# Loading six fields of one tile in parts of 39, 40 and 49 rows in a DMA-bound pairwise-product kernel

## The chip, the cores and the metric

The kernel runs on one core of a Trainium2 chip. Times are device microseconds (us) of that core, as medians of several executions; every execution that is compared here was in the fast state, with a granted TensorE clock of 0.535 to 0.548 in the profiled ones. A profile is one further execution.

## The reference

```python
# r_x: (4096, 32, 64) float32;  W: (64, 64) float32
vid = x @ W                                   # per field
out[:, pair(i, j), :] = x[:, i, :] * vid[:, j, :]   # all i < j: 496 pairs
# out: (4096, 496, 64) float32, 520 MB
```

(The two lines are the reference's content in short form.) The output is fifteen times the input: this is a problem of writing.

## The kernel before

The batch is cut into 16 tiles of 256 rows. A tile of x lies in SBUF as 128 partitions (two halves of the batch by 64 embedding positions) by 32 fields by 128 rows. (SBUF is the on-chip memory that DMA transfers fill and empty, PSUM the memory that TensorE writes.) TensorE makes `vid` for a tile in PSUM, VectorE multiplies, and SyncE issues the store of each finished piece. There are two x buffers and three output buffers.

```python
xpool = ctx.enter_context(tc.tile_pool(name="x", bufs=2))
opool = ctx.enter_context(tc.tile_pool(name="out", bufs=3))
...
def load(t, pieces, queue):
    xt = xpool.tile([P, F, C], F32, tag="x", name=f"x_{t}")
    n = F // pieces
    for lo in range(0, F, n):
        queue.dma_start(out=xt[:, lo : lo + n, :], in_=x[t][:, lo : lo + n, :])
    return xt

loaded = [load(0, 4, nc.sync), load(1, 2, nc.sync)]
...
for t in range(NT):
    if 0 < t < NT - 1:
        loaded.append(load(t + 1, 4, nc.scalar))
    xt = loaded[t]
    ...                                       # matmuls: vid
    for at, m, w, i, di, j, dj in products(by_field() if t < 2 else by_block()):
        ...
        nc.vector.tensor_tensor(o, left, right, ALU.mult)
        ...
        nc.sync.dma_start(out=out[t][:, sent:at, :], in_=ot[:, sent - base : at - base, :])
```

From tile 2 on a store moves 128 rows of 63,488 bytes. Each of the sixteen DMA engines takes eight of these rows, and each adds one step to the store's completion semaphore, the counter by which the program learns that a transfer has landed, after its eighth.

Of the kernel before, what the change touches and what calls it, by code (L numbers as in the profile page):

```python
# [1 line left out]

# [4 lines left out]

F32 = mybir.dt.float32
ALU = mybir.AluOpType

P = 128

C = 128

SLOT = 124

PAD = 8

GROWING = [
    21, 15, 19, 23, 27, 19, 29, 18, 19, 20, 38, 28, 24, 25, 47, 34, 29, 61,  # L20
    55, 69, 66, 58, 77, 47, 93, 31,
]


def by_field():

    return [("row", j, 0, 1, j) for j in range(1, 32)]


def by_block():  # L30


    def within(lo):
        yield "step", lo, 2, 1, 0
        for k in range(2):
            yield "step", lo, 4, 2, k
        for i in (lo, lo + 8):
            yield "row", i + 4, i, 4, 4
        yield "row", lo + 8, lo, 8, 8

    yield from within(0)
    yield "row", 16, 0, 16, 16
    yield from within(16)


def products(blocks):

    at = 0
    for kind, a, b, c, d in blocks:

        if kind == "row":
            rows, n, i0, di, j0, dj = c, d, b, 0, a, 1
        else:
            rows, n, i0, di, j0, dj = 16 // b, c, a, b, a + c + d, b
        r = k = 0
        while r < rows:
            room = SLOT - at % SLOT
            if k or room < n:
                m, w = 1, min(n - k, room)
            else:  # L60
                m, w = min(rows - r, room // n), n
            yield at, m, w, i0 + r * di + k, di, j0 + r * dj, dj
            at += m * w
            if w == n or k + w == n:
                r, k = r + m, 0
            else:
                k += w


def pairs(blocks):  # L70

    for at, m, w, i, di, j, dj in products(blocks):
        for r in range(m):
            for k in range(w):
                yield i + r * di + k, j + r * dj


@with_exitstack
def pairwise_bilinear_kernel(
    ctx: ExitStack,  # L80
    tc: tile.TileContext,
    x: bass.AP,
    w: bass.AP,
    out: bass.AP,
):




    nc = tc.nc  # L90
    NT = x.shape[0]
    F = x.shape[2] - PAD
    D = P // 2
    NP = F * (F - 1) // 2

    BANK = 512 // C


    ctx.enter_context(tc.manual_schedule(engines={mybir.EngineType.SP}))

    const = ctx.enter_context(tc.tile_pool(name="const", bufs=1))
    xpool = ctx.enter_context(tc.tile_pool(name="x", bufs=2))
    opool = ctx.enter_context(tc.tile_pool(name="out", bufs=3))
    psum = ctx.enter_context(
        tc.tile_pool(name="ps", bufs=1, space=bass.MemoryType.PSUM)
    )
    vid = psum.tile([P, F, C], F32)


    w2 = const.tile([P, D], F32)  # L110
    nc.sync.dma_start(out=w2, in_=w)  # L111
# [5 lines that stand above are left out]
            queue.dma_start(out=xt[:, lo : lo + n, :], in_=x[t][:, lo : lo + n, :])  # L117
        return xt

    loaded = [load(0, 4, nc.sync), load(1, 2, nc.sync)]  # L120

    done = 0
    growing = iter(GROWING)
    until = next(growing)
# [6 lines that stand above are left out]
        for b in range(0, F, BANK):  # L131
            for h in range(2):
                half = slice(h * D, (h + 1) * D)
                nc.tensor.matmul(  # L134
                    vid[half, b : b + BANK, :],
                    lhsT=w2[half, :],
                    rhs=xt[half, b : b + BANK, :],
                    start=True,
                    stop=True,
                )  # L140

        sent = 0
        for at, m, w, i, di, j, dj in products(by_field() if t < 2 else by_block()):
            base = at - at % SLOT
            if at == base:
                ot = opool.tile([P, SLOT, C], F32, tag="o", name=f"o_{t}_{at}")
            n = m * w
            o = ot[:, at - base : at - base + n, :]
            if m == 1:
                left = xt[:, i : i + w, :]  # L150
                right = vid[:, j : j + 1, :].to_broadcast([P, w, C])
            else:
                o = o.rearrange("p (m w) c -> p m w c", m=m)
                right = vid[:, j : j + (m - 1) * dj + 1 : dj, :].unsqueeze(2).to_broadcast([P, m, w, C])
                if di == 0:
                    left = xt[:, i : i + w, :].unsqueeze(1).to_broadcast([P, m, w, C])
                else:
                    left = xt.rearrange("p (m d) c -> p m d c", d=di)[:, i // di : i // di + m, i % di : i % di + w, :]
            nc.vector.tensor_tensor(o, left, right, ALU.mult)  # L159
            at += n  # L160
            if t * NP + at == until or at in (base + SLOT, NP):
                nc.sync.dma_start(
                    out=out[t][:, sent:at, :],
                    in_=ot[:, sent - base : at - base, :],
                )
                sent = at
                if t * NP + at == until:
                    until += next(growing, NT * NP)


_INS = ["r_x", "L0_rec_W"]
_OUTS = [((4096, 496, 64), "float32")]


# [36 lines left out]
```

## Time and profile before

| | before |
|---|---|
| median of the first 3 runs | 1293.61 us (1291.99 to 1294.53) |
| profiled run, time / span | 1295.21 us / 1293.4 us |
| DMA engines covered by packets, both data queues | 99.5% |
| VectorE busy | 1083.6 us, 84% |
| first / last of the last store's sixteen steps | 1282.40 / 1292.58 us |

The first line was all that was known of the kernel's own spread when the prediction was made. The last line is the one to remember: the sixteen engines end up to 10.2 us apart, and the kernel ends with the last of them. Below, an engine's **lag** is its step of a store behind the first engine's step of the same store. The prediction shows the lines of the profile for this.

### The profile page before, as it was taken

To read this page: it belongs to the slowest core of one execution; us is meant where nothing else is said; L and a number is where in the kernel's file an instruction comes from. 1 tells how busy PE (TensorE), PEld (TensorE's weight loads), DVE (VectorE), ACT (ScalarE), POOL (GpSimd) and SP (SyncE) were. 2 spreads that over 40 slices of the span, in tenths; PEclk is the share of its full clock that TensorE was granted. 3 is DMA by queue.
4 is the path that set the end of the run, shared out by engine and by line. 5 is a ranking of instruction groups with operands and counts; after the bars stand their busy time and mean duration, and the time that the engine had idled before them with its cause. 6 is when DMAs were issued, how large, how long until landed. Compare 5 with 4: busy or idle time off the path is not lost.

```text
span 1293.4 us, 1789 instructions
## 1 busy us (share of the span) xinstructions
PE 227.8 (18%) x512; PEld 48.5 (4%) x512; DVE 1083.6 (84%) x320; POOL 0.2 (0%) x4
## 2 busy tenths in 40 slices
PE   4112122112122121221212212122121221212000
PEld 1000000000000000000000000000000000000000
DVE  7999999888898887888879788798887988979870
POOL 0000000000000000000000000000000000000000
PEclk7555555555555565555555556555565555555555
DMA  9999999999999999999999999999999999999996
GB/s 393 429 423 438 429 432 435 430 431 434 433 434 431 432 433 435 433 435 436 433 431 436 431 433 431 435 434 431 431 431 434 431 433 427 427 431 438 438 430 302
DMA packets 20889, 553.80 MB, mean 428 GB/s; under 512 B 2448, under 2 KB 2448, under 8 KB 10256
## 3 DMA queue, kind: packets, MB, share of 16 engines
q1 hardware_dynamic: 12816, 524.33, 93.9%
q10 hardware_dynamic: 8064, 29.36, 5.6%
q8 instruction: 4, 0.07, 0.0%
q14 instruction: 5, 0.04, 0.0%
HBM read 33.59 MB, written 520.09 MB: 428 GB/s over the span
## 4 chain that ended last, share of the span: by engine, by line
DMA 55%; DVE 39%; issue 2%; PE 0%; DVEq 0%; SPq 0%
DMA out_dram<-o 55%; DVE o L159 39%; DMA x<-in_r_x_dram 0%; PE vid L134 0%; DVEq L200 0%; DVEq L159 0%; SPq L111 0%
## 5 line engine op out<-in xcount | busy, mean ns | idle before, releaser
L159 DVE TENSOR_TENSOR o<-x,vid 128x2048 f32<-128x2048 f32 (+13 forms) x320 | 1083.6, 3454 | 170.0 <-DMA out_dram<-o 124.2
L134 PE MATMUL vid<-x,w 64*64 64x512 f32 x512 | 227.8, 1025 | 958.6 <-DMA x<-in_r_x_dram 629.4
L134 PEld LDWEIGHTS vid<-x,w 64*64 64x64 f32 x512 | 48.5, 205 | 1136.2 <-DVE o L159 572.9
L182 POOL MEMSET const-bfloat16-1.0<- 128x1 bf16 x1 | 0.1, 102 | 0.0
L182 POOL MEMSET const-uint8-127<- 128x1 uint8 x1 | 0.1, 101 | 0.0
L182 POOL MEMSET const-float32-0.0<- 128x1 f32 x1 | 0.1, 99 | 0.2 <-issue 0.2
L182 POOL MEMSET const-float32-1.0<- 128x1 f32 x1 | 0.1, 98 | 0.0
## 6 DMA issues: line engine op xcount, KB each, us to landing
out_dram<-o SPq DMA_DIRECT2D x56, 7936.0 KB, 43.1
x<-in_r_x_dram ACTq DMA_DIRECT2D x56, 512.0 KB, 45.5
out_dram<-o SPq DMA_DIRECT2D x2, 3008.0 KB, 17.7
out_dram<-o SPq DMA_DIRECT2D x1, 5952.0 KB, 26.9
out_dram<-o SPq DMA_DIRECT2D x1, 4928.0 KB, 23.1
out_dram<-o SPq DMA_DIRECT2D x1, 4416.0 KB, 19.0
out_dram<-o SPq DMA_DIRECT2D x1, 4224.0 KB, 21.2
out_dram<-o SPq DMA_DIRECT2D x1, 3904.0 KB, 15.3
```

Source lines behind the costliest of these rows:

```text
L134: nc.tensor.matmul(vid[half, b : b + BANK, :], lhsT=w2[half, :], rhs=xt[half, b : b + BANK, :], start=True, stop=True,)
L159: nc.vector.tensor_tensor(o, left, right, ALU.mult)
L182: nc = _bacc.Bacc("TRN2", target_bir_lowering=False, num_devices=1, dynamic_dma_scratch_size=1024)
```

## The change

The change gives some engines more of an early load than others. Tile 1's x was two loads of 128 rows, eight rows an engine in each. Now 26 of its 32 fields are one load of 128 rows, and the other six come in parts of 39, 40 and 49 rows, which are not shared over all sixteen engines.

```diff
-    loaded = [load(0, 4, nc.sync), load(1, 2, nc.sync)]
+    loaded = [load(0, 4, nc.sync)]
+
+    x1 = xpool.tile([P, F, C], F32, tag="x", name="x_1")
+    for p, q, lo, hi in ((0, P, 6, F), (0, 39, 0, 6), (39, 79, 0, 6), (79, P, 0, 6)):
+        nc.sync.dma_start(out=x1[p:q, lo:hi, :], in_=x[1][p:q, lo:hi, :])
+    loaded.append(x1)
```

## The prediction

> **What bounds the kernel now.** I read the page first: the busy lines, the forty slices, the queue table, the grouped instructions. Busiest engine and data movement come out like this:
>
> ```profile
> PE 227.8 (18%) x512; PEld 48.5 (4%) x512; DVE 1083.6 (84%) x320; POOL 0.2 (0%) x4
> ...
> DMA  9999999999999999999999999999999999999996
> ...
> q1 hardware_dynamic: 12816, 524.33, 93.9%
> q10 hardware_dynamic: 8064, 29.36, 5.6%
> HBM read 33.59 MB, written 520.09 MB: 428 GB/s over the span
> ```
>
> VectorE has 16% to spare; the sixteen DMA engines have nothing: 93.9 + 5.6 = 99.5% of their span is covered by packets. q1 is SyncE's queue (all stores, tile 0's and tile 1's x), q10 is ScalarE's (x of tiles 2 to 15). To see where the missing share lies I cut the span into stretches. Columns: length, busy us of each engine, TensorE clock, DMA share, GB/s.
>
> ```profile
> 0.00:3.00 3.00, 0.00 (x0) 0.00 (x0) 0.00 (x0) 0.20 (x4) 1.00 0.31 60
> 3.00:12.00 9.00, 6.87 (x24) 2.35 (x26) 4.25 (x7) 0.00 (x0) 1.00 1.01 415
> 12.00:60.00 48.00, 10.65 (x34) 2.12 (x30) 48.00 (x24) 0.00 (x0) 0.57 1.01 428
> 60.00:212.00 152.00, 29.86 (x66) 5.97 (x68) 151.87 (x57) 0.00 (x0) 0.53 1.01 434
> 212.00:1280.00 1068.00, 180.48 (x392) 38.10 (x392) 879.47 (x234) 0.00 (x0) 0.54 1.00 433
> ```
>
> From 3 us on the DMA share is 1.00 or a hair over (packets overlap by some ns at hand-over). Every stretch in which something waits (VectorE for buffers, TensorE for x) is one in which the transfers run at full rate. The end is different:
>
> ```profile
> 1278.00:1280.00 2.00, 0.00 (x0) 0.00 (x0) 0.00 (x0) 0.00 (x0) 0.50 1.17 508
> 1280.00:1282.00 2.00, 0.00 (x0) 0.00 (x0) 0.00 (x0) 0.00 (x0) 0.50 0.66 286
> 1282.00:1284.00 2.00, 0.00 (x0) 0.00 (x0) 0.00 (x0) 0.00 (x0) 0.50 0.30 127
> 1284.00:1286.00 2.00, 0.00 (x0) 0.00 (x0) 0.00 (x0) 0.00 (x0) 0.50 0.29 127
> 1286.00:1288.00 2.00, 0.00 (x0) 0.00 (x0) 0.00 (x0) 0.00 (x0) 0.50 0.22 95
> 1288.00:1290.00 2.00, 0.00 (x0) 0.00 (x0) 0.00 (x0) 0.00 (x0) 0.50 0.07 32
> 1290.00:1292.00 2.00, 0.00 (x0) 0.00 (x0) 0.00 (x0) 0.00 (x0) 0.50 0.00 0
> ```
>
> (A packet counts where it begins, so the shares are coarse.) All work but the last store's data is done, and the engines finish one after another. The trace has each engine's own step of the store's completion semaphore. For the last store they fall at 1282.4 (seven engines within 0.25 us), 1284.0 to 1284.2 (four), then 1288.2, 1288.5, 1288.9, 1289.3, and the last alone at 1292.6. The first store's sixteen steps lie within 0.86 us. So one engine ends 10.2 us after the best, and the end of the kernel is that engine's end: 2.6 us of start, its packets back to back, the completion.
>
> The chain of waits says the same from the other side:
>
> ```profile
> 1197.35 39.09 DMA out_dram<-o
> 1236.49 0.04 issue
> 1236.53 0.69 DVE o L159
> 1237.22 1.13 DVEq L200
> 1238.35 15.25 DVE o L159 x5
> ```
>
> VectorE resumes at 1236.5, when the last of the sixteen steps of a store issued 39 us earlier has come (1226.3 to 1236.4).
>
> **What the Trainium skill says.** "DMA: Bandwidth & Descriptors", section "Why a DMA increments its semaphore by 16 and not by 1": the number k of engines is the largest up to 16 that divides the slowest dimension of both sides, and from the sync and scalar queues they are the lowest-numbered k. Hence 39 rows go to 13 engines (three each), 40 to 10 (four each), 49 to 7 (seven each). All transfers of the kernel before have 128 rows, so its trace can't confirm this for other counts; it agrees for 128 (sixteen steps each). Same page, "Queues, rings and completion order": an engine takes turns between queues packet by packet. The trace agrees: an x load of tile 2 or later, eight 4096-byte packets an engine, takes 45.5 us to land because each packet sits between stores of 2346 ns. Same page, "Latency and other measured facts": engines 7 and 15 are usually slower than the others; here some engines do fall behind, but the trace has no engine numbers to check which.
>
> **The change, part by part.** Bytes are equal. Removed: two loads of 128 rows by 8192 bytes. Added: one of 128 rows by 26 fields (13312 bytes) and parts of 39, 40 and 49 rows by 6 fields (3072 bytes). Packet durations in the trace: 4096 bytes 159 ns, 8192 bytes 309 ns, so 0.0366 ns a byte. Estimates from these: 13312 bytes 309 + 5120 x 0.0366 = 497 ns; 3072 bytes 159 - 1024 x 0.0366 = 122 ns.
>
> Each engine's time on this tile before: 16 x 309 = 4944 ns. After, 8 x 497 = 3976 ns plus its small rows:
> - engines 0 to 6: 3 + 4 + 7 = 14 rows, 1708 ns: 5684, that is +0.74 us
> - engines 7 to 9: 3 + 4 = 7 rows, 854 ns: 4830, -0.11 us
> - engines 10 to 12: 3 rows, 366 ns: 4342, -0.60 us
> - engines 13 to 15: none: 3976, -0.97 us
>
> The sum over sixteen is nearly 0 (5.18 - 0.33 - 1.80 - 2.91 = +0.14 us). As every engine is busy to its own end, an engine's shift at 13 us is carried to the end, and the kernel's end moves by the shift of the one engine that is last. It has 3.3 us on the next, so no other can take its place.
>
> SyncE issues two more loads at about 0.45 us each. Before, its last load was issued at 3.69 us and the first store, waiting for VectorE, at 11.14: hidden.
>
> The order of instructions shows one more effect. Eight completion semaphores are used in turn, and a DMA waits until the one eight places earlier in program order has landed. With two more DMAs the turn shifts, and the scheduler also places the loads of tile 2 slightly differently. The store issued at 84.26 us now waits for the first of those loads, which landed at 91.80; the next store waits for the second load, which was behind the first. So one store is issued about 8 us late, and its predecessor's data ends at 90.2 to 91.6. SyncE's queue would be empty for 1 to 3 us. But the other three pieces wait in ScalarE's queue: 24 packets x 159 ns = 3.8 us for each engine, which now go without stores between them. The gap is filled by work that has to be done anyway. From tile 3 on, the waits are the old ones under other names.
>
> **The rivals.**
> - The late engine is one of 13 to 15: -0.97 us, 1292.6. For: the parts give most to seven engines, and seven are the early ones at the end. Against: the trace doesn't number them.
> - It is one of 0 to 6: +0.74 us, 1294.3.
> - The engines relieved run dry in the first 30 us. For: stores there come barely in time. The fifth is issued at 22.85; from the first load's issue (1.17) to the first packets of x (about 2.3) is about 1 us, so it is ready at 23.9, and the fourth begins to land at 24.82. An engine that is 0.97 us ahead arrives at 23.85. Idle would be at most some tenths, and only an engine that is ahead has it: it reduces the -0.97, no more.
> - The late store at 84 us starves VectorE: a buffer is freed late. VectorE's later use of that buffer begins at about 128 us, and its second store landed at 112.8. With 15 us to spare I expect nothing; if the fill failed, 2 to 3 us would be lost, 1296.
> - Full balance of the lag. The mean lag of the last store's sixteen steps is (7 x 10.1 + 4 x 8.5 + 4.4 + 4.1 + 3.7 + 3.3) / 16 = 7.5 us, 0.6%. That is the most that any sharing could bring; this one moves 0.97 us.
>
> **Range and chances.** I weigh engines 13 to 15 with 0.4, 10 to 12 with 0.15, 7 to 9 with 0.2, 0 to 6 with 0.25: -0.39 - 0.09 - 0.02 + 0.19 = -0.3 us. From 1293.61: 1293.3 us. The runs of before spread from 1291.99 to 1294.53, more than the effect, so a median of a few may be 1 us off by chance; with the shift of -1.0 to +0.7 I take 1291.5 to 1295.1. Two per cent are 26 us. Nothing found comes near: full balance saves 7.5, a failed fill costs 3. Faster 0.01, within 0.98, slower 0.01.
>
> **What would show it right or wrong.** Right: in the changed kernel the three parts have 13, 10 and 7 steps that come with data and the rest at once; the steps of the first store spread over about 2 us in place of 0.86, in groups of 7, 3, 3, 3; the DMA share stays 1.00 from 3 to 1280 us, also at 84 to 95; the tile 2 loads land ten or more us earlier; the last store still has one engine some 9 to 11 us behind, within 1 us of before. Wrong: a share well under 1 anywhere between 12 and 100 us; VectorE waiting longer for buffers around 128 us; or the lag of the last engine changing by much more than 1 us, which would mean that the lag isn't carried along but depends on what the engines do together.

## The result, and the profile after

Four runs of each kernel: changed 1297.49 us median (1296.89 to 1299.03), before 1294.07 us (1291.99 to 1296.55). The ratio is 1.0027 with a 95% interval of 1.0007 to 1.0048. Ratios here are the mean time of one kernel's fast runs over that of the other's of the same rounds, so they are not quite the ratio of the medians quoted beside them. By the 2% criterion that is the same time, as predicted, but 1297.49 lies 2.4 us above the top of the predicted range.

The page of the changed kernel, its DMA slices and queues:

```profile
DMA  9999999999999999999999999999999999999995
...
q1 hardware_dynamic: 12830, 524.33, 93.7%
q10 hardware_dynamic: 8064, 29.36, 5.6%
```

The same bytes in 14 packets more; only the last slice differs. The changed kernel cut into stretches (columns as in the prediction: length, busy us of PE, PEld, DVE, POOL, TensorE clock, DMA share, GB/s):

```profile
3.00:12.00 9.00, 6.53 (x20) 2.23 (x22) 3.90 (x7) 0.00 (x0) 1.00 1.01 407
12.00:60.00 48.00, 11.89 (x38) 2.56 (x34) 48.00 (x24) 0.00 (x0) 0.59 1.01 425
60.00:120.00 60.00, 12.86 (x32) 2.68 (x32) 60.00 (x32) 0.00 (x0) 0.56 1.02 429
120.00:212.00 92.00, 15.24 (x32) 2.86 (x32) 92.00 (x26) 0.00 (x0) 0.52 1.00 432
212.00:1280.00 1068.00, 180.37 (x392) 38.16 (x392) 879.74 (x235) 0.00 (x0) 0.54 1.00 433
```

No stretch from 3 to 1280 us is idle, and VectorE is busy throughout from 12 to 212 us: it waits for no buffer there. The predicted late store is there: over 76 to 96 us SyncE's waits for a load of x, first of the kernel before, then of the changed one (in total, times, longest):

```profile
SPq L162 <- DMA x<-in_r_x_dram: 7.2, 1, 7.2
```

```profile
SPq L167 <- DMA x<-in_r_x_dram: 16.1, 2, 15.4
```

The store that was issued at 84.26 us is now issued at 92.48. In its place tile 2's loads pass, which over 70 to 130 us show as follows (last column: median us from issue to landing), before and then changed:

```profile
x<-in_r_x_dram ACTq DMA_DIRECT2D x4, 512.0 KB, 29.8
```

```profile
x<-in_r_x_dram ACTq DMA_DIRECT2D x4, 512.0 KB, 16.8
```

The pieces had landed at 91.8, 101.4, 113.0 and 124.3 us; now they land at 91.7, 93.1, 95.0 and 96.7. Chaining the packets in time (each begins within some ns of its predecessor's end on the same engine) gives whole-DMA idle time between 4 and 1270 us: 0.00 us an engine before, 0.01 after. So no engine was without a packet. But a packet can hold a wait. From 84 to 95 us the DMA share is 1.00 in both kernels while the bytes differ, before and then changed:

```profile
84.00:95.00 11.00, 3.06 (x8) 0.84 (x8) 11.00 (x8) 0.00 (x0) 0.50 1.00 426
```

```profile
84.00:95.00 11.00, 2.45 (x6) 0.84 (x8) 11.00 (x8) 0.00 (x0) 0.50 1.00 401
```

The store whose data end there has rows of 31,232 bytes. In the kernel before, fifteen of the sixteen last rows took 1156 to 1158 ns, one 1220. In the changed one, with the next store late, thirteen of them took 1352 to 2028 ns, and by and large the earlier an engine began its row, the longer the row. Over that store's 128 rows this is 0.3 us an engine more than before (0.55 against 0.24 us over 1156 ns a row). The even kernel even9, with the same late store, shows it too (0.64 us).

Otherwise the pair of profiles differs in the views at the end. The changed kernel's last 14 us:

```profile
1280.00:1282.00 2.00, 0.00 (x0) 0.00 (x0) 0.00 (x0) 0.00 (x0) 0.50 1.10 476
1282.00:1284.00 2.00, 0.00 (x0) 0.00 (x0) 0.00 (x0) 0.00 (x0) 0.50 0.44 190
1284.00:1286.00 2.00, 0.00 (x0) 0.00 (x0) 0.00 (x0) 0.00 (x0) 0.50 0.37 159
1286.00:1288.00 2.00, 0.00 (x0) 0.00 (x0) 0.00 (x0) 0.00 (x0) 0.50 0.15 63
1288.00:1290.00 2.00, 0.00 (x0) 0.00 (x0) 0.00 (x0) 0.00 (x0) 0.50 0.07 32
1290.00:1292.00 2.00, 0.00 (x0) 0.00 (x0) 0.00 (x0) 0.00 (x0) 0.50 0.07 32
1292.00:1294.00 2.00, 0.00 (x0) 0.00 (x0) 0.00 (x0) 0.00 (x0) 0.50 0.07 32
```

A share of 0.07 is the one packet of one engine of sixteen that begins in the slice. Before, it ended in the slice from 1288 us; now one engine alone starts packets for six us. The last store's steps say it exactly: first step 1283.18 (before 1282.40), last 1296.15 (before 1292.58). The first engines are 0.8 us later, and the last engine's lag is 12.97 us in place of 10.19.

**How the lag comes about.** Two things can be read from the packets, and neither was in the prediction. A store's row of 63,488 bytes takes 2342 ns. On an engine that is behind, some rows take over 2400 ns (most of these up to 2515), and mostly it is the eighth, the last row of a store: 176 of 197 such rows in the kernel before, 159 of 184 in the changed one. The share of slow last rows by the engine's lag at its step of the store before, from about 130 us on (the table needs each engine followed from packet to packet, so it is a reconstruction; the lower three rows are of kernels that are described below):

```
lag, us        0-0.3    0.3-0.8   0.8-1.5   1.5-2.3   2.3-3
before         0%       8%        64%       28%       56%
changed        0%       2%        31%       42%       67%
even9_again    1%       12%       14%       8%        10%
uneven7        2%       2%        8%        5%        17%
burden         0%       2%        16%       23%       43%
```

(In the kernel before, 1 of 453 in the first column.) The last engine of before had 52 slow rows, 42 of them eighth rows, 7.3 us in sum over 2342 ns a row; that of the changed kernel 64, 45 of them eighth rows, and 9.4 us. These sums are most of the two lags. The second thing is smaller: the page's two queues called instruction (nine packets of 8192 or 16,384 bytes in the whole run) put 0.3 or 0.9 to 1.0 us on whichever engine carries one. Slow last rows are rare at lags under 0.3 us and common in these two kernels above 0.8, but there is no fixed threshold: in burden two engines stayed at 1.0 to 1.2 us from 260 to 500 us and did not grow.

### The profile page after: what moved, and what is told of

The parts are those of the page before. It is cut to its first block, busy times and chain, and to the rows that moved or that the text cites. A ratio compares the mean times of both kernels' runs of the same rounds, so it can differ in the third digit from the quotient of the medians.

```text
span 1297.1 us, 1792 instructions
## 1 busy us (share of the span) xinstructions
PE 226.9 (17%) x512; PEld 48.5 (4%) x512; DVE 1083.6 (84%) x320; POOL 0.2 (0%) x4
## 4 chain that ended last, share of the span: by engine, by line
DMA 59%; DVE 36%; issue 2%; PE 0%; DVEq 0%; SPq 0%
DMA out_dram<-o 58%; DVE o L164 36%; DMA x<-in_r_x_dram 0%; PE vid L139 0%; DVEq L205 0%; DVEq L164 0%; SPq L111 0%
```

## The experiments

Four sets, each on one chip with eleven runs of the kernel before beside it, in alternation. The theories at the start: the imposed shares set which engine lags and how much (**sharing**, theory 1 in the recorded texts); more loads and another turn of the completion semaphores cost the time (**count**, theory 2); and, from the second set on, these kernels differ by nothing that the runs can tell (**chance**, theory 3). Theory 1' is sharing with a threshold of about 0.8 us of lag, from which an engine falls back further.

### Even parts: even9

Parts of 48, 32 and 48 rows are shared evenly by sixteen engines; everything else is as in the changed kernel, its late store included (issued at 93.03 us).

```diff
-    ... ((0, P, 6, F), (0, 39, 0, 6), (39, 79, 0, 6), (79, P, 0, 6)):
+    ... ((0, P, 6, F), (0, 48, 0, 6), (48, 80, 0, 6), (80, P, 0, 6)):
```

> The changed kernel with its three small parts cut at 48, 32 and 48 rows, so that all sixteen engines get three, two and three rows: the same bytes, sizes, number of loads and semaphore waits, shared evenly. If the uneven sharing costs the 3.4 us (theory 1: engines that start behind fall further behind), this is back at the time before, 1293 to 1295 us. If the two extra loads, the shifted semaphores and the store that is issued 8 us later cost it (theory 2), it is as slow as the changed kernel, 1296.5 to 1298.5.

1293.99 us median (1291.13 to 1297.67, 6 runs), ratio 0.9984 (0.9966 to 1.0001). The kernel before in the same rounds: 1297.21 us median, from 1290.84 to 1298.32. Two findings: more loads and the late store cost nothing that this shows, so **count** is weak; and the kernel before, whose three first runs lay within 2.5 us, spreads over 7.5.

### Fewer loads, uneven and even: uneven7, even7

Tile 0's x in two loads (8 and 24 fields) instead of four, so that the number of loads is again that of the kernel before; once with the uneven and once with the even parts.

```diff
-    loaded = [load(0, 4, nc.sync)]
+    loaded = [load_two(0)]          # fields 0-8, then 8-32
```

> The changed kernel, uneven parts included, with tile 0's x in two loads in place of four, so that seven loads come ahead of the stores as before, and no store is issued late for a load. Theory 1 (sharing): 2 to 4 us slower than before, 1296 to 1298. Theory 2 (number of loads and waits): as before, 1293 to 1295.

1297.02 us (1291.48 to 1298.76), ratio 0.9994 (0.9973 to 1.0014). The median lies where **sharing** expected it, but so does that of the kernel before in the same rounds, 1297.21.

> The control for uneven7: tile 0's x in two loads, the small parts of tile 1 shared evenly. Both theories: as before, 1293 to 1295.5; its difference to uneven7 is the sharing alone: 2 to 4 us under theory 1, under 1 under theory 2.

1295.7 us (1290.83 to 1297.72), ratio 0.9985 (0.9966 to 1.0004). The uneven kernel is not slower than the one before, and it differs from its even twin by 0.6 us in the mean, less than its own runs differ. Both still have the late store (issued at 92.26 and 93.05 us), against what was expected, so the fewer loads did not undo that. The profiled run of the uneven one took 1292.1 us and is worth a look, because it has the sharing of the changed kernel and not its tail:

```profile
1280.00:1282.00 2.00, 0.00 (x0) 0.00 (x0) 0.00 (x0) 0.00 (x0) 0.50 0.88 381
1282.00:1284.00 2.00, 0.00 (x0) 0.00 (x0) 0.00 (x0) 0.00 (x0) 0.50 0.73 317
1284.00:1286.00 2.00, 0.00 (x0) 0.00 (x0) 0.00 (x0) 0.00 (x0) 0.50 0.30 127
1286.00:1288.00 2.00, 0.00 (x0) 0.00 (x0) 0.00 (x0) 0.00 (x0) 0.50 0.15 63
1288.00:1290.00 2.00, 0.00 (x0) 0.00 (x0) 0.00 (x0) 0.00 (x0) 0.50 0.00 0
```

Everything has begun by 1288 us. Its last store's steps run from 1283.29 to 1289.40: the first engine ends as in the changed kernel, the lag is 6.1 us in place of 13.0.

### Another distance of the output rows: outpad

Is the slow last row a matter of the address that follows? The kernel before, with 4 KB more between the output's rows.

```diff
-        laid = (NT, 2 * D, shape[1], C)
+        laid = (NT, 2 * D, shape[1] + PAD, C)
```

> The kernel before with the output's rows 8 fields (4 KB) further apart in HBM, the result cut out by a slice. The engines that end late lose their time in the last of each store's eight packets, 2450 ns in place of 2342. If that depends on how the addresses of the late engine's last row and the other engines' next rows lie to each other (theory A), the slow packets are fewer and the kernel takes 1285 to 1291. If it comes from the engine or the completion itself (theory B), 1292.5 to 1295.5 as before.

1296.88 us (1294.42 to 1297.7), ratio 0.9999 (0.9986 to 1.0012). The slow last rows are still there, 48 of over 2400 ns on the last engine, with 6.5 us. The theory of addresses falls for this distance.

### The changed kernel again, and all fields uneven: after_again, full

The first is the changed kernel without an edit. The second has all 32 fields of tile 1 in parts of 39, 40 and 49 rows.

```diff
-    ... ((0, P, 6, F), (0, 39, 0, 6), (39, 79, 0, 6), (79, P, 0, 6)):
+    ... ((0, 39, 0, F), (39, 79, 0, F), (79, P, 0, F)):
```

> The changed kernel unaltered, to be timed beside eleven runs of the kernel before, which by now has shown 1290.8 to 1298.3 us on the chip of the first experiments. If the 3.4 us of the first measurement belong to the change (theories 1 and 2), this is again 2 to 5 us slower than the runs of before beside it. If the first four runs against four were drawn from one wide spread (theory 3), it lies within 1.5 us of them, either side.

1296.27 us (1294.51 to 1299.84), ratio 1.0002 (0.9982 to 1.0022): the 3.4 us of the first comparison are not there.

> All 32 fields of tile 1 in parts of 39, 40 and 49 rows (no even load at all): engines 0 to 6 get 14 rows of 16 KB in place of 8, 3.7 us more, engines 13 to 15 get none, 4.9 us less. Five times the change's unevenness. If a shift is carried to the end (the prediction's step), the median is 2.5 to 5 us above the runs of before; if it also grows (theory 1), 5 to 12 us. If it is worn off on the way or the end is set by something else (theory 3), within 1.5 us.

1298.35 us (1297.25 to 1299.09, 5 runs), ratio 1.0017 (1.0001 to 1.0034): over the kernel before by 1.4 us in the median and 2.2 in the mean, under what a carried or growing shift was expected to cost, and not clearly zero. Its stretches show where the shift went:

```profile
3.00:30.00 27.00, 16.58 (x46) 4.94 (x47) 22.12 (x19) 0.00 (x0) 0.79 0.98 367
...
72.00:79.00 7.00, 1.97 (x4) 0.29 (x4) 7.00 (x8) 0.00 (x0) 0.50 0.87 346
```

Here DMA engines are idle: counted from the packets, 0.66 us an engine up to 30 us and 1.75 us from there to 150. The engines ahead wait for work at 72 to 79 us while the others catch up. And its rows of 16,384 bytes took 907 ns in the mean, the fastest 611, which is 2.4 us an engine. The profiled run's last store has a lag of 8.4 us, less than the changed kernel's, but its first engine ends at 1287.9.

### Which engine is it: mark_before, mark_after, mark_even9

The trace has no engine numbers. Seven tiny loads at the very end, of 14, 12 and so on to 2 rows, go to the lowest-numbered 14, 12, ... engines by the rule that the prediction cites, so an engine's count of tiny packets tells its number within a pair.

```diff
+    for k in (14, 12, 10, 8, 6, 4, 2):
+        mark = const.tile([P, C], F32, tag=f"mark{k}", name=f"mark{k}")
+        nc.sync.dma_start(out=mark[:k, :], in_=x[0][:k, 0, :])
```

> The kernel before with seven tiny loads (512 bytes a row) behind its last store, of 14, 12, 10, 8, 6, 4 and 2 rows, one row an engine: the count of tiny packets at the end of an engine's work tells which pair of engines it is. Time: as before within 1.5 us. If the late engine is among 13 to 15 the prediction's first rival is met, if among 0 to 6 the second; theory 1 needs the late engine of this and of the changed kernel to be in a group that the change gives more to.

1296.56 us (1294.28 to 1297.63), ratio 1.0003 (0.9987 to 1.0019).

> The changed kernel with the same seven tiny loads behind the last store. Time: as the changed kernel within 1.5 us, so a second sample of it: 2 to 5 us above before under theories 1 and 2, within 1.5 us under theory 3. The late engine should be one of 0 to 6 under theory 1; under theory 3 it may be any, the same as without the change or not.

1297.84 us (1296.68 to 1299.78), ratio 1.0017 (1.0001 to 1.0033), 2.2 us over the kernel before in the mean: more than **chance** expected (within 1.5).

> The even control (parts of 48, 32 and 48 rows, same number of loads as the changed kernel) with tiny loads of 14 to 2 rows at the end. Its engines should lie as in mark_before: one or both of 14 and 15 and one of 12 and 13 last, 6 to 10 us behind the best. If instead one of 2 and 3 is last as in mark_after, the exchange of places comes from the number of loads and not from the sharing. Time: within 1.5 us of before.

1295.57 us (1292.05 to 1298.75), ratio 0.9993 (0.9972 to 1.0015). The engines with the largest lags, at three moments (following an engine from store to store is a reconstruction from packets that touch):

```
before + marks          21 us   ~143 us   end
14 or 15                0.79    0.65      8.79
12 or 13                0.79    0.63      8.68   (instruction fetch at 178 us)
2 or 3                  0.30    1.22      7.01   (at 84, 501 and 923 us)
14 or 15, the other     0.77    0.66      6.71

changed + marks         21 us   ~144 us   end
12 or 13                0.71    1.60     10.68   (at 83 us)
2 or 3                  0.66    1.92     10.65   (at 501 and 927 us)
4 or 5                  1.77    0.98      6.14   (at 298 us)
14 or 15                1.29    0.13      4.18   (at 444 us)
14 or 15, the other     0.29    0.13      0.13
0 or 1, both     1.59 / 1.46   0.29/0.25  0.72 / 0.25
```

In the changed kernel two things in the table are uncertain. The two last engines end 0.03 us apart, so their histories may be exchanged; and the first column gives one of 14 and 15 a lag of 1.29 us and one of 2 and 3 only 0.66, which does not fit the shares of 13 to 15 and of 0 to 6, so engines may have been confused at 84 to 103 us. The last column depends only on the tiny packets at the end.

In the kernel before the last engine is one of 14 and 15, as the prediction's first rival supposed (13 to 15), with one of 12 and 13 right behind it. In the changed kernel 14 and 15 end 4.2 and 0.1 us behind in place of 8.8 and 6.7, far more than the 0.97 us taken from them, and others are last. Engines 0 and 1, two of the seven that were given most, start 1.5 us behind and end among the first: between 84 and 103 us, where SyncE's queue runs dry and the tile 2 loads pass, most lags of that kind vanish. The unmarked changed kernel shows the same without engine numbers: of the seven engines that were 1.37 to 1.74 us behind at 22 us, six were 0.2 to 0.4 us behind at 104 us, and the seventh, at 1.67, had carried an instruction packet at 83 us. In the even kernel with marks it was again one of 12 and 13 (9.0 us).

### Burdening and relieving on purpose: burden, relief, after_third

If a lag over 0.8 us grows, then putting one on a single engine should make that engine last (`burden`), and taking 0.6 us from the engines 12 to 15 should help (`relief`). `after_third` is the changed kernel once more.

```diff
 # burden (with marks)
+    ... ((0, 112, 0, F), (112, 126, 0, F), (126, 127, 0, F), (127, P, 0, F)):
 # relief
+    ... ((0, P, 16, F), (0, 96, 0, 16), (96, 120, 0, 16), (120, P, 0, 16)):
```

> Tile 1's x in parts of 112, 14, 1 and 1 rows by 32 fields (16 KB, 0.61 us a row): engine 0 gets ten rows in place of eight, 1.2 us more, engines 14 and 15 seven, 0.6 us less, all others as before; tiny loads of 15, 14, 13, 12, 3, 2 and 1 rows at the end number the engines. In mark_before engines 0 and 1 ended first (0 to 0.6 us behind the best), 14 and 15 ended 8.8 and 6.7 us behind. If a shift is carried (the prediction's step), engine 0 ends 1.2 to 2 us behind and 14 and 15 about 8.2 and 6.1. If an engine that is more than about 0.8 us behind falls back further with each store and one that is less doesn't (theory 1'), engine 0 ends 5 to 10 us behind and 14 and 15 under 3.5. Time: within 2 us of before either way.

1304.04 us (1301.45 to 1305.1), ratio 1.0056 (1.0039 to 1.0074), 7.4 us in the mean. The test failed for its purpose:

```profile
60.00:72.00 12.00, 1.97 (x4) 0.29 (x4) 12.00 (x4) 0.00 (x0) 0.50 1.02 439
72.00:79.00 7.00, 1.97 (x4) 0.29 (x4) 7.00 (x8) 0.00 (x0) 0.50 0.42 139
```

The DMA engines stood at 0.42 for 7 us, 3.9 us of pause (0.58 x 7 is 4.1): the scheduler placed tile 2's loads earlier in the turn of semaphores, and a store issued at 64 us in the kernel before waited for them until 80.86. The pause also took away the imposed lags: the steps of the first store spread over 3.1 us, but at 132 us no engine was more than 1.05 us behind, and the burdened one, by the reconstruction, 0.32; it ended at 0.25. The other half of the loss is in the loads: the rows of 16,384 bytes took 1095 ns in the mean, the fastest 611, 3.9 us an engine more. So the run shows what slow load rows and an empty store queue cost together, and tells nothing about a burden put on one engine.

> A try at a better sharing: 16 fields (8 KB, 0.31 us a row) in parts of 96, 24 and 8 rows, so engines 12 to 15, which start 0.6 to 0.8 us behind in mark_before, get six rows in place of eight (0.62 us less), engines 0 to 7 nine (0.31 us more, from at most 0.4), 8 to 11 eight. Under theory 1' engines 12 to 15 stay under the 0.8 us and no other is lifted over it, except by an instruction fetch; the last engine is then one with an early fetch, and the median is 1 to 4 us below before. Under the carried shift 0.3 to 0.6 us below; theory 3: within 1 us.

1299.22 us (1298.2 to 1300.1), ratio 1.002 (1.0004 to 1.0036): a miss. Relieving the engines that were late in the kernel before made it slower, 2.7 us in the mean. Its loads show a cost that was not expected: the 8192-byte rows took 309 ns in the load of 128 rows, but 544 in the mean in the parts of 96, 24 and 8 rows, which is 1.9 us an engine. In its profile an engine with instruction fetches at 82, 502 and 926 us, 1.73 us behind at 22 us, ends 12.04 us behind.

> The changed kernel unaltered, a third sample. So far it took 3.4 us more than before beside four runs, 0.3 to 0.6 us more beside eleven, and with the tiny loads at the end 2.2 us more. A true cost of about 2 us (late engines that relieve and load exchange places, and grow) gives 1 to 3 us above the eleven runs of before here; no cost at all (theory 3) gives 1 us either side.

1298.38 us (1295.07 to 1299.41), ratio 1.0012 (0.9994 to 1.003): 1.6 us over the kernel before in the mean, where a true cost was expected (1 to 3); the interval still includes no cost.

### The sharing against chance, side by side: after_fourth, even9_again, uneven7_again, even7_again

After three sets the kernels with uneven parts had 28 runs, mean 1297.24 us, those with even parts 18 runs, mean 1295.09. That looked like a case for **sharing**, pooled over chips and rounds. The last set put the four kernels beside each other on one chip, unedited.

> The changed kernel once more, now beside its even twin on the same chip in the same rounds. Sharing theory (the uneven sharing costs about 2 us, through the lag of the last engine): 2.2 us over the even twin with eight loads of x, and 1.0 to 2.0 us over the kernel before. Chance theory (the pooled difference is the spread of eight us that all these kernels have): within 0.7 us of the even twin and of the kernel before.

1294.19 us (1292.6 to 1296.44), ratio 0.9998 (0.9982 to 1.0015).

> Parts of 48, 32 and 48 rows in place of 39, 40 and 49, the same number of loads, the same late store at 92 to 93 us. Sharing theory: 2.2 us below the changed kernel of the same rounds, 0 to 1.5 us below the kernel before. Chance theory: within 0.7 us of both.

1295.0 us (1294.19 to 1299.38), ratio 1.001 (0.9993 to 1.0028).

> The uneven parts with tile 0 in two loads: six early loads of x in place of eight. Sharing theory: like the changed kernel, 1 to 2 us over the kernel before and 2 us over its even twin. If the number of loads or the turn of the semaphores is what counts beside the sharing: like its even twin, 1 to 2 us below the changed kernel. In the first set this kernel was 0.3 us below the kernel before and 0.6 us over its even twin, which left the question open.

1294.99 us (1292.01 to 1296.89), ratio 1.0001 (0.9984 to 1.0019).

> Even parts with tile 0 in two loads. Sharing theory: 2 us below the uneven twin and like the even twin with eight loads of x. Chance theory: within 0.7 us of all the others.

1296.31 us (1291.14 to 1298.72), ratio 1.0012 (0.999 to 1.0034). The kernel before: 1294.65 us (1290.66 to 1298.1, 11 runs). Now the uneven kernels are the faster ones by 1.4 to 1.6 us in the mean. That answers the set's question against **sharing** as a cause of 2 us: the order turned round. All runs together (mean, and the difference with about 95% of uncertainty from the scatter of single runs):

```
before                      48 runs  1295.64 us, standard deviation 2.18, 1290.66 to 1298.72
changed, unedited           22 runs  1296.55 us, standard deviation 2.18   +0.9 +- 1.1
  without the first four    18 runs  1296.29 us (before, 44 runs: 1295.77) +0.5 +- 1.3
uneven parts (see below)    40 runs  1296.41 us                            +0.8 +- 1.0
even parts                  30 runs  1295.43 us                            -0.2 +- 1.1
uneven minus even                                                          +1.0 +- 1.1
```

(Differences are to the kernel before, but for the last row. The row of uneven parts is the 22 unedited runs, the marked kernel's six and the twelve with fewer loads; full, burden and relief are left out.) No version beat both kernels.

## Why the prediction was right or wrong

**Right.** The kernel is bound by its DMA engines to the end. The parts have 13, 10 and 7 steps that come with data and the others at once, which is the rule cited from the Trainium skill, "DMA: Bandwidth & Descriptors", section "Why a DMA increments its semaphore by 16 and not by 1", now seen for three further row counts. The first store's steps spread over 1.81 us (predicted about 2; before 0.86), and seven of them stand together at its end (1.48 to 1.81 us); the three groups of three cannot be told apart. The late store came with the predicted 8 us, and no engine was without a packet, though the rows around 90 us were longer. In the kernel before the last engine was one of 14 and 15 in the marked run. Class: within 2%.

**Wrong: the steps that gave the number.** The measured median is 4.2 us from the predicted one. With the means over all runs that is about 2.0 us (1295.64 against the 1293.61 that it started from), 1.2 us (+0.9 in place of -0.3) and 0.9 us (the four runs against the mean of 22). So:

1. The start and the width. "A median of a few may be 1 us off by chance" rested on three runs within 2.5 us. The kernel's single runs have a standard deviation of 2.2 us and range over 8. The start lay 2 us low, the four runs of the result 1 us high. How they came to lie so is luck. That the range left no room for it is the main failure, and it is most of the 3.4 us of the first comparison with it: later sets of the unedited changed kernel found +0.6, +1.6 and -0.2 us in the mean.

2. "An engine's shift at 13 us is carried to the end." It is not. "Busy to its own end" was true, but it does not follow that every engine needs the same time for the same packets. In the changed kernel's profile the rows of 22 to 105 us took, over the usual time of their size, 1.3 to 1.6 us in sum on the five engines furthest ahead, and 0.2 to 0.5 us on six of the seven that were behind (1.2 on the seventh). So most of the imposed shift was gone by 104 us, and afterwards the lags grew by slow rows. In sixteen profiles that could be followed, the largest lag at 143 us says little about the end: 1.67 us became 13.00 in the changed kernel, 2.68 became 6.14 in uneven7, and in after_fourth an engine at 0.20 became the last, with 10.62. The average does rise: engines without a later instruction fetch that were under 0.6 us behind at 143 us ended 0.6 us behind (100 engines), those at 0.8 to 1.6 us 4.4 (23), those above 6.3 (6).

3. "It has 3.3 us on the next, so no other can take its place." The marks show others taking it. In eight of the sixteen profiles the last engine was not the one with the largest lag at 143 us.

4. The packets. 3072 bytes were estimated at 122 ns. The fastest took 121, but the mean was 160 in the changed kernel's profile (146 to 184 in the twelve profiles with such rows, even parts included). With the 13,312-byte rows at 503 ns in place of 497 and the first loads a little slower, the loads of tiles 0 and 1 take 11.13 us an engine in place of 10.59, +0.54 where the sum said +0.14. Together with the 0.3 us of the long rows around 90 us this is the 0.8 us by which the first step of the last store is later. Every profile with the six fields in parts, even or uneven, shows it: this first step falls at 1282.9 to 1283.3 us, against 1282.4 to 1282.6 in before, outpad and mark_before.

**What sets the time of a run.** This is the mechanism that the runs do show, because it needs no comparison of kernels:

```
                 first step   last step    lag   time of that run
uneven7            1283.29     1289.40    6.1    1292.1
uneven7_again      1283.15     1290.37    7.2    1293.09
even9_again        1283.08     1291.53    8.5    1294.38
mark_before        1282.64     1291.43    8.8    1294.28
before             1282.40     1292.58   10.2    1295.21
after_fourth       1282.93     1293.56   10.6    1296.44
even9              1283.06     1294.59   11.5    1297.43
after              1283.18     1296.15   13.0    1299.03
after_third        1283.18     1296.53   13.3    1299.37
```

The time is the last step plus 2.6 to 2.9 us in every row. The first step moves by 0.9 us over all of them, the lag by 7, and even and uneven kernels stand mixed in the list. Four profiles are of the changed kernel itself (the three here and after_again: first step 1283.11, lag 11.9, time 1297.9). Their first steps lie within 0.3 us, and their times of 1296.4 to 1299.4 follow the lag, 10.6 to 13.3. So in the profiled runs of one kernel the spread is the last engine's lag. (even7, even7_again and outpad fit the rows too. In full, relief and burden the first step itself is late: 1287.92, 1283.81 and 1290.82.)

**What stays open.** Whether the unevenness of the parts costs anything: uneven minus even, +1.0 +- 1.1 us, does not exclude 0 or 2. full and relief, with larger shifts, lay 2.2 and 2.7 us over the kernel before in the mean of one set each; in full idle time and slow load rows come to 4.8 us an engine, more than the loss; in relief the slow load rows are 1.9 us of it. Why rows loaded in parts are slow was not tested: uneven sharing is not needed for it, as the even parts have it too. Why a store's last row is slow on an engine that is behind: not the output's row distance; nothing else was tried with success. Burdening one engine without emptying the queue was not achieved. So what is shown is that the prediction started from three runs out of a wide spread, and that the last engine's lag makes the spread; what makes one run's lag 6 us and another's 13 is not.

## What to carry to other kernels

When sixteen DMA engines are busy to the end, look at the steps of the last completion semaphore, not only at the average: the slowest engine is the time. A DMA share of 1.00 does not show that nothing waits: look at the GB/s and at the time of one row as well. Before predicting tenths of a per cent, measure the spread of the kernel you start from; three runs that agree within 2.5 us can belong to a spread of 8, and a change of under 1 us then needs dozens of runs. A difference that is found after pooling should be tested once more with the rivals side by side before it is told as a cause.

## What the Trainium skill lacked or had wrong

- "DMA: Bandwidth & Descriptors", "Latency and other measured facts", has engines 7 and 15 as usually slower, and puts that, as a best guess, down to transfers issued from GpSimd. This kernel issues none, so the runs don't test the guess. With marks, the late engines of the kernel before were both 14 and 15, one of 12 and 13, and one of 2 and 3 (6.7 to 8.8 us behind); 6 and 7 were not (0.1 and 1.5 us). In the changed kernel 14 and 15 ended at 4.2 and 0.1 us. No fixed engine is the slow one here.
- The same page doesn't say that an engine which has fallen behind can go on falling: the last of its eight 63,488-byte rows of a store often takes over 2400 ns in place of 2342, at lags of 0.8 to 2.3 us in 5 to 64% of the stores of five profiles, at lags under 0.3 us in at most 2%.
- "Runtime: NRT & Kernel Launch", section "Instruction fetch mechanics", has fetches in blocks of 16 KiB, by DMA, and the cost of crossing into a new block, for the instruction stream, as mostly hidden. It doesn't say what a fetch does to a DMA engine that is busy throughout. Here packets of the instruction queues keep such an engine for 0.31 us (8192 bytes) or 0.88 to 0.97 us (16,384 bytes), nine in a run, and the engine that has one is that much later.
- No page that I found has the time of one row in a load of part of the 128 rows: 3072 bytes took 146 to 184 ns in the mean, in even and uneven parts, where a line through 4096 and 8192 bytes gives 122; 8192 bytes took 544 ns in the mean in relief's parts, and 309 in a load of 128 rows.
